# Decoder of two layers: the norms of the first cross attention moved to ScalarE, one turn later in the windowed attention, and the token shift of the last layer by transfers

## The chip, the cores and the metric

The kernel runs on one core of one Trainium2 chip. The metric is the device time of one execution in microseconds (us), the median of several runs. The engines of the core are TensorE (PE, with its weight loads PEld), VectorE (DVE), ScalarE (ACT), GpSimd (POOL) and SyncE (SP, which here only issues transfers).

## The reference

A post-norm decoder with two layers computes on `x` of 4 x 512 tokens of 128 features, with a context of 4 x 32 tokens. `_layernorm` subtracts the mean of the features and divides by the root of the variance plus 1e-5.

```
x = _layernorm(x + mamba(x))               # selective scan
x = _layernorm(x + cross_attention_0(x, ctx))
x = _layernorm(x + moe(x))                 # a shared expert and 2 of 8
x = _layernorm(x + windowed_attention(x))  # 16 heads, window 128
x = _layernorm(x + cross_attention_1(x, ctx))
x = _layernorm(x + local_layers(x))        # 2 layers, window 64
```

Three parts matter here. The first cross attention normalizes its input, attends with 16 heads to 32 context tokens, and adds a gated result:

```
xn = layernorm(x) * ln_gamma + ln_beta
out = softmax((xn @ w_q) . k * scale) . v @ w_out + b_out
x = _layernorm(x + out * tanh(gate))
```

The windowed attention gives for each tile of tokens an output by features, with the sum of the weights beside it, by which it is divided. Each of the two local layers has a feed-forward part that begins with a token shift and a norm:

```
def shift_token(t):
    t1, t2 = jnp.split(t, 2, axis=-1)
    t2 = jnp.pad(t2, ((0, 0), (1, 0), (0, 0)))[:, :-1]
    return jnp.concatenate([t1, t2], axis=-1)

h = shift_token(x); h = layernorm(h) * lg + lb
x = x + ffn(h)
```

So the second half of the features of a token comes from the token before it.

## The kernel before, in words

Tokens lie on the 128 partitions, 16 tiles of 128 tokens (`NT`), four tiles (`NJ`) to a batch; the features lie along the row. A matmul needs its contraction on the partitions, so tiles are turned by TensorE (`TE.transpose` with `ident`) into PSUM and copied from there by ScalarE or VectorE. All three parts are written in `tc.manual_schedule()`: each engine takes its instructions in about the order in which the code issues them, short ones slipped between long ones, and an engine that meets an instruction whose input is late stands still with all that is queued behind it.

*First cross attention* (`xa` pool, lines 971 to 1095). Each step `k` of 19 runs `tile_a(k)` and `tile_b(k)`: score of tile `k+1`, largest and exponentials of `k`, sums and products of `k-1`, turn and values of `k-2`, result of `k-3`. Beside these the next batch is prepared: `stats_x` (mean and variance of a tile on VectorE, `bn_stats`, `bn_aggr`, and `ve`, variance plus 1e-5; then the root `rs` on GpSimd by `rpow`, line 157, and `xr`, the residual plus bias, line 977), `norm_x` (line 985, VectorE: subtract the mean, multiply by the root; line 986: turn into `ptx`), and behind the fourth tile `xT` (ScalarE, line 989). Batch 0 is prepared in the stage before. `result` (line 1031) adds the residual and takes `stats` of the sum, `norm_r` (line 1036, VectorE) writes the normalized tile to `x2`. `exponentials` uses ScalarE (line 1004), `sums` multiplies by the inverse on GpSimd (`xpr`, line 1013), `turned_` turns that (`pt`, line 1019) and copies it on ScalarE (`xpT`, line 1021). A list `aside` adds the routing of the experts and the shared expert (`ph`, `w2s`) to the later steps; GpSimd then scatters the tokens of the first half to their experts (`xs`, line 818), and the first `fetch` of the experts (`xg`, turned in `ptg`, line 912) waits for all 16 scatters.

*Windowed attention* (lines 1157 to 1360). Step `s` takes four heads of tile `s // 4`. It issues `scores(s+1)` (`psc`, and VectorE's `nm`, line 1243), `tails(s, 0)`, `exponentials(s+1)` (`pe`, ScalarE, line 1250), `weights(s)` (turn `ptp`, line 1260, then `pT`, line 1262, one half on VectorE and one on ScalarE), `values(s-1)` (`pa`), `tails(s, 1)`, and the preparation `made` of the next batch, among it the rotary matmuls `pq` at s mod 16 of 5, 6, 7 and 9. `tails` finishes the tile before in four steps: `gathered` (ScalarE, `ao`, line 1280), `by_tokens` (turn `pn`, line 1288; inverse `rc`, line 1291; product `at`, line 1293), `by_features` with `output`, and `normed`. `pn`, `pto`, `po`, `pq` and `pv` share one PSUM buffer (tag `pm`).

*Last layer* (lines 1391 to 1792). Step `g` takes half the heads of tile `g // 2`; `around` and `feed` are lists of what else is issued at the three places of a step: the projections `pqk` and `pv` with the transfers `vh<-va` on SP (lines 1426 and 1428), the rotary parts on VectorE and GpSimd, the turns `ptk` (line 1485) and `ptq` (line 1476), the output `po` and its sum `xa` (VectorE, line 1561), and the feed-forward of the batch before. That begins with `ff_shift`: `shifted` turns the four tiles of `xa` to features (`pts`, line 1799); ScalarE copies the first 64 features (`hT`, line 1801) and VectorE the other 64, one token later (line 1802). One place later `ff_tokens` turns it back (`pth`, line 1578; copy to `hn`, line 1580). Then come `ff_stats` (with `rs` and two products `mr` on GpSimd, lines 157, 198, 199), `ff_norm` (ScalarE, line 209), `ff_features`, `ff_gates`, `ff_hidden` (`pff`, `ge`) and `ff_out` (`pof`). The last of the 8 turns of two layers and four batches runs alone behind the loop. The turns, `po`, `pv` and `pff` share three PSUM buffers (tag `pt`).

Helpers that the change uses: `shifts(mv, rs)` computes minus mean times root for four tiles on GpSimd, and `normal(x, mv, rs, of, mr)` normalizes four tiles by four ScalarE activations with that as bias and the root as scale.

Of the kernel before, what the change touches and what calls it, by code (L numbers as in the profile page):

```python
# [11 lines left out]
F32 = mybir.dt.float32  # L12
BF16 = mybir.dt.bfloat16
I32 = mybir.dt.int32
AF = mybir.ActivationFunctionType
ALU = mybir.AluOpType
# [3 lines left out]
P = 128  # L20
B, T, D = 4, 512, 128
NJ = T // P
# [35 lines left out]
def decoder_kernel(ctx: ExitStack, tc: tile.TileContext, a: dict):  # L58
    nc = tc.nc
    V, S, G, TE = nc.vector, nc.scalar, nc.gpsimd, nc.tensor  # L60
# [32 lines left out]
    def vcol(name, i=0):  # L93
        o = _VEC[name][0] + i
        return vec[:, o:o + 1]
# [59 lines left out]
    def rpow(out, in_, n):  # L155

        G.tensor_tensor(out, in_, cneg.to_broadcast([P, n]), ALU.pow)  # L157

    def stats(src):

        st = sm.tile([P, 6], F32, tag="st", name="st")
        V.bn_stats(st, src)
        mv = sm.tile([P, 2], F32, tag="mv", name="mv")
        V.bn_aggr(mv, st)
        ve = sm.tile([P, 1], F32, tag="ve", name="ve")
        V.tensor_scalar_add(ve, mv[:, 1:2], 1e-5)  # L166
        rs = sm.tile([P, 1], F32, tag="rs", name="rs")
        rpow(rs, ve, 1)
        return mv, rs
# [25 lines left out]
    def shifts(mv, rs):  # L195

        mr = sm.tile([P, NJ], F32, tag="mr", name="mr")
        G.tensor_tensor(mr, mv[:, :, 0], rs, ALU.mult)
        G.tensor_tensor(mr, mr, cminus.to_broadcast([P, NJ]), ALU.mult)
        return mr  # L200
# [715 lines left out]
    def weights(hf, t):  # L916

        ex = nc.values_load(which[hf][0:1, t:t + 1], engines=[mybir.EngineType.DVE], min_val=0, max_val=7,
                            skip_runtime_bounds_check_because="a minimum bounds the number by 7")
        wts[hf, t] = gp.tile([P, 2, 512], F32, tag="wt", name="wt", bufs=3)  # L920
        V.tensor_copy(wts[hf, t], w12[:, bass.ds(ex, 1)].rearrange("p o w h -> p (o w) h"))
# [47 lines left out]
            store(hf, g)  # L969

    with tc.tile_pool(name="xa", bufs=3) as t1:
        xrs, mvs, ptx, xTs, scs, mxs, xes, rcs, prs, xpTs, rs_ = ({} for _ in range(11))

        def stats_x(i):
            mvs[i] = stats(x1[:, i, :])
            xrs[i] = t1.tile([P, D], F32, tag="xr", name="xr", bufs=8)
            G.tensor_tensor(xrs[i], x1[:, i, :], gb, ALU.add)

        def norm_x(i):
            b, j = divmod(i, NJ)  # L980
            if j == 0:
                ptx[b] = ps.tile([P, NJ, P], F32, tag="ph", name="ptx")
            mv, rs = mvs.pop(i)
            xn = t1.tile([P, D], F32, tag="xn", name="xn")
            V.tensor_scalar(xn, x1[:, i, :], mv[:, 0:1], rs, ALU.subtract, ALU.mult)
            TE.transpose(ptx[b][:, j, :], xn, ident)
            if j == NJ - 1:
                xTs[b] = t1.tile([P, T], F32, tag="xT", name="xT", bufs=2)
                S.activation(xTs[b], ptx.pop(b).rearrange("p j t -> p (j t)"), AF.Identity,
                             bias=vcol("ln_b"), scale=vcol("ln_g"))  # L990

        def score(i):
            b, j = divmod(i, NJ)
# [35 lines left out]
        def result(i):  # L1029
            r = rs_[i] = t1.tile([P, D], F32, tag="r", name="r")  # L1030
            V.scalar_tensor_tensor(r, pos_.pop(i), gate, xrs.pop(i), ALU.mult, ALU.add)
            mvs["r", i] = stats(r)

        def norm_r(i):
            mv, rs = mvs.pop(("r", i))
            V.tensor_scalar(x2[:, i, :], rs_.pop(i), mv[:, 0:1], rs, ALU.subtract, ALU.mult)

        def tile_a(k):

            nxt = (k // NJ + 1) * NJ  # L1040
            if k + 1 < NT:
                score(k + 1)
            if 0 <= k - 2 < NT:
                turned_(k - 2)
            if k < NT:
                largest(k)
            if 0 <= k - 3 < NT:
                result(k - 3)
            if nxt < NT:
                for j in ((0, 1), (2, 3), (), ())[k % NJ]:  # L1050
                    stats_x(nxt + j)

        def tile_b(k):
            nxt = (k // NJ + 1) * NJ
            if k < NT:
                exponentials(k)
            if 0 <= k - 1 < NT:
                sums(k - 1)
            if 0 <= k - 3 < NT:
                norm_r(k - 3)  # L1060
            if 0 <= k - 2 < NT:
                values(k - 2)
            if nxt < NT:
                for j in ((), (0, 1), (2, 3), ())[k % NJ]:
                    norm_x(nxt + j)


        aside = {(7, 1): [(turn, 0)], (8, 1): [(shared_first, 0)], (9, 1): [(shared_second, 0), (shared_add, 0)],
# [88 lines left out]
    with tc.tile_pool(name="wa", bufs=2) as bp, tc.tile_pool(name="wa_p", bufs=2) as t1, \  # L1157
# [150 lines left out]
        def normed(i):  # L1308
# [4 lines left out]
        made = {3: [(turn_x,)], 5: [(rotary, 0, 0)], 6: [(rotary, 0, 1)], 7: [(rotary, 1, 0)], 9: [(rotary, 1, 1)],  # L1313
                10: [(head_values,)], 11: [(head_keys, 0), (head_keys, 1)], 12: [(head_keys, 2), (head_keys, 3)],
                13: [(head_keys, 4), (head_keys, 5)], 14: [(head_keys, 6), (head_keys, 7)]}
        tail = [[None, gathered], [by_tokens, None], [by_features, output], [normed, None]]

        def tails(s, k):
            i = s // 4 - 1
            f = tail[s % 4][k]  # L1320
            if f and i >= 0:
                f(i)

        with tc.manual_schedule():
            beside = {3: [(blocks_x, 1)], 5: [(g_x, 0)], 6: [(g_x, 1)], 7: [(g_x, 2)], 9: [(g_x, 3)], 10: [(v_x, 0), (v_x, 1)],
                      11: [(v_x, 2)], 12: [(v_x, 3)]}
            blocks_x(0)
            for t in sorted(made):
                for f, *c in made[t]:
                    f(0, *c)  # L1330
                for f, *c in beside.get(t, []):
                    f(*c)
            scores(0)
            exponentials(0)
            last = 4 * NT
            for s in range(last):
                if s + 1 < last:
                    scores(s + 1)
                tails(s, 0)
                if s + 1 < last:  # L1340
                    exponentials(s + 1)
                weights(s)

                if s < HT_:
                    for q in range(2):
                        gather(1, 2 * s + q)
                if s % 2 == 0 and 4 <= s < 4 + 2 * HT_:
                    combined(1, s // 2 - 2)
                if s % 2 and 4 <= s < 4 + 2 * HT_:
                    norm_3(1, s // 2 - 2)  # L1350
                if s:
                    values(s - 1)
                tails(s, 1)
                if s // 16 + 1 < B:
                    for f, *c in made.get(s % 16, []):
                        f(s // 16 + 1, *c)
            values(last - 1)
            for s in range(last, last + 4):
                tails(s, 0)
                tails(s, 1)  # L1360

    kept.close()

# [27 lines left out]
    with tc.tile_pool(name="la_b", bufs=2) as bp, tc.tile_pool(name="la_t", bufs=2) as t1, \  # L1391
# [1 line left out]
            tc.tile_pool(name="la_ps", bufs=2, space=PSUM) as ps:  # L1393


        hTz = [bp.tile([P, T], F32, tag=f"hT{k}", name=f"hT{k}", bufs=1) for k in range(3)]
        for k in hTz:
            V.memset(k[64:128, 0:1], 0.0)
        va = bp.tile([P, NJ, 8, 65], F32, tag="va", name="va", bufs=1)
# [5 lines left out]
        ins = [x5]  # L1405
        hTs, pqks, tas, tbs, rns, sss, qTs, pes, pTs, ats, aTs = ({} for _ in range(11))
        xTs, xes, xps, xpTs = ({} for _ in range(4))
        xas, h2s, hns, hnTs, xabs, ges, mvs, fins = ({} for _ in range(8))


        def shift(b):
# [149 lines left out]
            V.tensor_tensor(xas[i // NJ][:, i % NJ, :], po, ins[i // NT][:, i % NT, :], ALU.add)  # L1561

        def ff_shift(q):
            l, b = divmod(q, B)
            xa = xas.pop(q)
            h2s[q] = hTz[2]
            shifted(nc, ps, xa, 0, h2s[q], ident, 3)
            xabs[q] = bp.tile([P, NJ, D], F32, tag="xab", name="xab", bufs=2)
            G.tensor_tensor(xabs[q], xa,
                            rcol("f_b2", 128 * l, 128).unsqueeze(1).to_broadcast([P, NJ, D]), ALU.add)  # L1570
            if l == 1:
                G.tensor_tensor(xabs[q], xabs[q], x5[:, b * NJ:(b + 1) * NJ, :], ALU.add)

        def ff_tokens(q):
            pt = ps.tile([P, NJ, P], F32, tag="pt", name="pth", bufs=3)
            hT = h2s.pop(q)
            for j in range(NJ):
                TE.transpose(pt[:, j, :], hT[:, j * P:(j + 1) * P], ident)
            hns[q] = bp.tile([P, NJ, D], F32, tag="hn", name="hn", bufs=1)
            S.copy(hns[q], pt)  # L1580

        def ff_stats(q):
            mv, rs = stats4(hns[q])
# [114 lines left out]
        def x_norm(b):  # L1698
# [14 lines left out]

        feed = {(0, 0): [[], [], [(ff_hidden, 2, 0)]], (0, 1): [[], [(ff_hidden, 2, 1)], []],
                (1, 0): [[(ff_shift, 1)], [(ff_hidden, 2, 2)], []],
                (1, 1): [[(ff_tokens, 1)], [], []],
                (2, 0): [[(ff_stats, 1)], [(ff_out, 2)], []],
                (2, 1): [[], [], [(ff_norm, 1)]],
                (3, 0): [[(last_stats, 2)], [], []],
# [11 lines left out]
        with tc.manual_schedule():  # L1731
# [46 lines left out]
            ff_shift(e)  # L1778
            for c in range(3):
                ff_hidden(e - 1, c)  # L1780
            ff_tokens(e)
            ff_stats(e)
            ff_out(e - 1)
            ff_norm(e)
# [10 lines left out]
def shifted(nc, ps, x, b, hT, ident, bufs):  # L1795

    pt = ps.tile([P, NJ, P], F32, tag="pt", name="pts", bufs=bufs)
    for j in range(NJ):
        nc.tensor.transpose(pt[:, j, :], x[:, b * NJ + j, :], ident)
    pf = pt.rearrange("p j t -> p (j t)")  # L1800
    nc.scalar.copy(hT[0:64, :], pf[0:64, :])
    nc.vector.tensor_copy(hT[64:128, 1:T], pf[64:128, 0:T - 1])
# [131 lines left out]
```

## Time and profile before

| | |
|---|---|
| three runs | 1275.3, 1281.07 and 1281.63 us, median 1281.07 |
| the profiled execution | 1280.2 us, span from the first to the last instruction 1278.5 us |
| mean granted clock of TensorE | 0.943 |
| busy in the span | PE 1100.2 us (86%), PEld 712.8 (56%), DVE 910.4 (71%), ACT 729.9 (57%), POOL 638.2 (50%) |
| chain that ended last, by engine | PE 49%, DVE 16%, ACT 6%, POOL 2%, issue 2% |

The stages that the change touches lie at about 315 to 425 us (first cross attention), 556 to 800 (windowed attention) and 870 to 1278 (last layer). A busy time counts what an engine does, not what bounds the stage: that is read from the waits (engine, line, what released it) and from the chain, which is followed back from the last instruction to what released each. A duration in a view by lines is a mean over all of that line's shapes.

### The profile page before, as it was taken

How to read it: one execution, taken by the hardware profiler on the slowest of the kernel's cores; microseconds unless marked ns; L12 is line 12 of the kernel's file. 1: busy time of each engine (PE TensorE's matmuls, PEld its weight loads, DVE VectorE, ACT ScalarE, POOL GpSimd, SP SyncE). 2: the span in 40 equal slices, each digit the busy share in tenths (PEclk: the TensorE clock that was granted, in tenths of full speed). 3: DMA queues.
4: the chain of work that ended last, by engine and by line, in shares of the span. 5: the costliest groups of instructions: out<-in, count | busy, mean ns of one | idle time of the engine just before them, and what ended most of it. 6: DMA issues, size and time to landing. Idle time of an engine off the chain costs nothing.

```text
span 1278.5 us, 22122 instructions
## 1 busy us (share of the span) xinstructions
PE 1100.2 (86%) x8429; PEld 712.8 (56%) x8429; DVE 910.4 (71%) x1722; ACT 729.9 (57%) x1612; POOL 638.2 (50%) x509
## 2 busy tenths in 40 slices
PE   4879888787698789988898998778999999999985
PEld 1334433343366779855555565446666566666563
DVE  3889898897876556847866666687777667766743
ACT  5696958662353445544656565346676665665752
POOL 3568675864546143433110100467785666676621
PEclk9799989897798899989999999899999999999997
DMA  9000000001200612200000000000110100110100
GB/s 270 1 0 1 1 0 1 1 0 65 84 1 30 228 63 80 63 22 14 2 1 2 2 2 2 0 9 21 28 23 14 27 22 15 26 23 14 35 14 17
DMA packets 34573, 38.92 MB, mean 30 GB/s; under 512 B 3378, under 2 KB 25667, under 8 KB 33987
## 3 DMA queue, kind: packets, MB, share of 16 engines
q1 hardware_dynamic: 31874, 31.69, 8.6%
q0 software_dynamic: 2048, 4.20, 1.1%
q10 hardware_dynamic: 544, 1.62, 0.5%
q8 instruction: 66, 1.08, 0.4%
q14 instruction: 41, 0.33, 0.1%
HBM read 20.80 MB, written 9.18 MB: 23 GB/s over the span
## 4 chain that ended last, share of the span: by engine, by line
PE 49%; DVE 16%; ACT 6%; issue 2%; POOL 2%; DMA 0%; DVEq 0%; ACTq 0%; POOLq 0%; SPq 0%
PE psc L189 9%; PE pa L189 4%; PE pqk L189 4%; PE pff L189 3%; PE po L189 3%; PE ptp L1260 3%; PE phg L189 3%; PE pog L189 2%; PE pv L189 2%; PE pof L189 2%; PE ptp L1527 1%; ACT pe L1250 1%; PE ptq L1476 1%; PE pq L189 1%; DVE nm L1243 1%
## 5 line engine op out<-in xcount | busy, mean ns | idle before, releaser
L440 POOL TENSOR_TENSOR h<-h,cb 128x1024 f32<-128x1024 f32 (+1 forms) x65 | 151.8, 2338 | 66.3 <-DVE h L435 49.8
L157 POOL TENSOR_TENSOR rs<-ve,cneg 128x1 f32<-128x1 f32 (+1 forms) x81 | 59.0, 728 | 232.5 <-DVE ve L166 193.8
L435 DVE TENSOR_TENSOR_SCAN h<-dA,pb 128x1024 f32<-128x1024 f32 x64 | 146.4, 2287 | 18.5 <-ACT dA L427 4.9
L1250 ACT ACTIVATE pe<-psc,nm 128x256 f32<-128x256 f32 (+1 forms) x256 | 93.6, 449 | 73.1 <-DVE nm L1243 72.8
L189 PE MATMUL y<-h,ident 128*128 128x512 f32 x256 | 127.2, 620 | 5.4 <-POOL h L440 4.7
L1458 POOL TENSOR_TENSOR ta<-ta,tb 128x1024 f32<-128x1024 f32 x32 | 75.4, 2357 | 111.6 <-DVE rc L1542 65.1
L1243 DVE TENSOR_REDUCE nm<-psc 128x4 f32<-128x1024 f32 (+1 forms) x64 | 69.8, 1091 | 56.7 <-PE psc L189 49.8
L157 POOL TENSOR_TENSOR rn<-ss,cneg 128x16 f32<-128x16 f32 x32 | 93.0, 2906 | 0.0
L1512 DVE TENSOR_REDUCE nm<-psc 128x4 f32<-128x512 f32 x64 | 44.0, 687 | 64.4 <-PE psc L189 62.7
L427 ACT ACTIVATE dA<-delta,negA 128x512 f32<-128x512 f32 (+1 forms) x128 | 85.3, 715 | 4.7 <-POOL delta L346 4.4
L189 PEld LDWEIGHTS y<-h,ident 128*128 128x128 f32 x256 | 49.6, 198 | 65.1 <-issue 46.5
L929 ACT ACTIVATE hTg<-phg,bias 128x128 f32<-128x128 f32 x184 | 52.7, 368 | 57.9 <-PE phg L189 57.2
L432 DVE TENSOR_TENSOR pb<-du,pb 128x1024 f32<-128x1024 f32 x64 | 77.5, 1211 | 2.7 <-PE pb L189 2.2
L1521 ACT ACTIVATE pe<-psc,nm 128x128 f32<-128x128 f32 x256 | 73.8, 381 | 5.4 <-DVE nm L1512 5.3
L189 PE MATMUL pb<-stk,sel 96*128 96x512 bf16 x128 | 41.5, 408 | 32.7 <-DVE h L435 15.5
L1260 PE MATMUL ptp<-ident,pe 128*128 128x128 f32 x448 | 64.5, 281 | 4.8 <-ACT pT L1262 2.0
L189 PE MATMUL pqk<-f_qkv,hT 128*128 128x512 f32 x128 | 64.9, 631 | 4.1 <-DVE tb L1452 4.0
L189 PE MATMUL psc<-kb,qk 64*128 64x256 f32 (+1 forms) x512 | 67.1, 381 | 0.0
L1466 POOL TENSOR_TENSOR ta<-ta,rn 128x1024 f32<-128x1024 f32 x32 | 60.9, 1903 | 2.4
L1260 PEld LDWEIGHTS ptp<-ident,pe 128*128 128x128 f32 x448 | 49.8, 142 | 16.9 <-issue 6.7
L189 PEld LDWEIGHTS <-sel 96*128 96x128 bf16 x192 | 18.9, 103 | 69.3 <-issue 42.3
L1432 ACT ACTIVATE sq<-pqk 128x1024 f32<-128x1024 f32 x32 | 32.9, 1029 | 42.8 <-PE pqk L189 35.3
(375 smaller groups left out, 2879.6 us busy)
## 6 DMA issues: line engine op xcount, KB each, us to landing
vh<-va SPq DMA_DIRECT2D x56, 130.0 KB, 2.3
w<-in_e_w_dram SPq DMA_DIRECT2D x16, 256.0 KB, 5.2
xs<-zero SPq DMA_DIRECT2D x2, 1472.0 KB, 12.7
xg<-xs SPq DMA_DIRECT2D x10, 256.0 KB, 3.1
ys<-yg SPq DMA_DIRECT2D x10, 256.0 KB, 2.4
f_qkv<-in_f_qkv_dram SPq DMA_DIRECT2D x1, 1536.0 KB, 6.6
x<-in_x_dram SPq DMA_DIRECT2D x4, 256.0 KB, 10.8
w_kv<-in_w_kv_dram SPq DMA_DIRECT2D x1, 1024.0 KB, 8.1
```

The source lines that it names most:

```text
L157: G.tensor_tensor(out, in_, cneg.to_broadcast([P, n]), ALU.pow)
L189: TE.matmul(out, lhsT=lhsT, rhs=rhs, start=start, stop=stop)
L427: S.activation(dAs[k % 4][:, c, c:T], delta[b % 2][:, c, c:T], AF.Exp, scale=negA[:, c * NST + n:c * NST + n + 1])
L432: V.tensor_tensor(pb, du[steps[k][0] % 2], pb, ALU.mult)
L435: V.tensor_tensor_scan(h.rearrange("p c t -> p (c t)"), dAs[k % 4].rearrange("p c t -> p (c t)"), pb.rearrange("p c t -> p (c t)"), 0.0, A ...
L440: G.tensor_tensor(h[:, c], h[:, c], cb.unsqueeze(1).to_broadcast([P, n, T]), ALU.mult)
L1243: V.tensor_reduce(nm, psc[:, :, 0:nk], AX.X, ALU.max, negate=True)
L1250: S.activation(pe[:, h, 0:nk], psc[:, h, 0:nk], AF.Exp, bias=nm[:, h:h + 1])
L1260: TE.transpose(ptp[:, h * nb + kk, :], pe[:, 2 * pr + h, kk * P:(kk + 1) * P], ident)
L1458: G.tensor_tensor(ta, ta, tbs.pop(i).rearrange("p w h d -> p (w h) d"), ALU.add)
L1466: G.tensor_tensor(ta, ta, rns.pop(i).unsqueeze(2).to_broadcast([P, 16, 64]), ALU.mult)
L1521: S.activation(pes[g][:, h, :], o[:, par, q, :], AF.Exp, bias=nm[:, k:k + 1])
```

## The change

Three edits in one. First cross attention: `stats_x` keeps mean and variance of the four tiles of a batch in one tile and takes one root and one `shifts` for all four behind the last; `norm_x` does a whole batch by `normal` on ScalarE at `tile_b` of the batch's second step, and the turn becomes `turn_x`, issued at `tile_a` of the third. The result's norm goes to ScalarE, with minus mean times root from two one-column products on GpSimd.

```
 def stats_x(i):
-    mvs[i] = stats(x1[:, i, :])
+    b, j = divmod(i, NJ)
+    if j == 0:
+        mvs[b] = sm.tile([P, NJ, 2], F32, tag="mv4", name="mv4")
+    st = sm.tile([P, 6], F32, tag="st", name="st")
+    V.bn_stats(st, x1[:, i, :])
+    V.bn_aggr(mvs[b][:, j, :], st)
     xrs[i] = t1.tile([P, D], F32, tag="xr", name="xr", bufs=8)
     G.tensor_tensor(xrs[i], x1[:, i, :], gb, ALU.add)
+    if j == NJ - 1:
+        ve = sm.tile([P, NJ], F32, tag="ve4", name="ve4")
+        V.tensor_tensor(ve, mvs[b][:, :, 1], eps.to_broadcast([P, NJ]), ALU.add)
+        rs = sm.tile([P, NJ], F32, tag="rs4", name="rs4")
+        rpow(rs, ve, NJ)
+        mvs[b] = mvs[b], rs, x1[:, b * NJ:(b + 1) * NJ, :], shifts(mvs[b], rs)

-def norm_x(i):
...
-    V.tensor_scalar(xn, x1[:, i, :], mv[:, 0:1], rs, ALU.subtract, ALU.mult)
-    TE.transpose(ptx[b][:, j, :], xn, ident)
...
+def norm_x(b):
+    xns_[b] = t1.tile([P, NJ, D], F32, tag="xn", name="xn", bufs=1)
+    normal(xns_[b], *mvs.pop(b))
+
+def turn_x(b):
+    pt = ps.tile([P, NJ, P], F32, tag="ph", name="ptx")
+    xn = xns_.pop(b)
+    for j in range(NJ):
+        TE.transpose(pt[:, j, :], xn[:, j, :], ident)
+    xTs[b] = t1.tile([P, T], F32, tag="xT", name="xT", bufs=2)
+    S.activation(xTs[b], pt.rearrange("p j t -> p (j t)"), AF.Identity, bias=vcol("ln_b"), scale=vcol("ln_g"))

 def result(i):
...
-    mvs["r", i] = stats(r)
+    mv, rs = stats(r)
+    mr = sm.tile([P, 1], F32, tag="mr1", name="mr1")
+    G.tensor_tensor(mr, mv[:, 0:1], rs, ALU.mult)
+    G.tensor_tensor(mr, mr, cminus, ALU.mult)
+    mvs["r", i] = mr, rs

 def norm_r(i):
-    V.tensor_scalar(x2[:, i, :], rs_.pop(i), mv[:, 0:1], rs, ALU.subtract, ALU.mult)
+    S.activation(x2[:, i, :], rs_.pop(i), AF.Identity, bias=mr, scale=rs)

 # tile_a
+        if k % NJ == 2:
+            turn_x(nxt // NJ)
 # tile_b
-        for j in ((), (0, 1), (2, 3), ())[k % NJ]:
-            norm_x(nxt + j)
+        if k % NJ == 1:
+            norm_x(nxt // NJ)
```

Windowed attention: `tails` has three places in a step, and `by_tokens` moves to the new one, behind `weights(s)` and ahead of `values(s-1)`.

```
-tail = [[None, gathered], [by_tokens, None], [by_features, output], [normed, None]]
+tail = [[None, None, gathered], [None, by_tokens, None], [by_features, None, output], [normed, None, None]]

 weights(s)
+tails(s, 1)
...
 values(s - 1)
-tails(s, 1)
+tails(s, 2)
```

Last layer: `ff_shift` writes the shifted tokens straight to `hn`, the second half of the features by two transfers on SP from partition to partition, the first half by a ScalarE copy; `ff_tokens` is gone, and `hn` has two buffers. The third `hT` buffer is gone. (The turns for the attention's own shift, `shift`, stay.)

```
 def ff_shift(q):
     l, b = divmod(q, B)
     xa = xas.pop(q)
-    h2s[q] = hTz[2]
-    shifted(nc, ps, xa, 0, h2s[q], ident, 3)
+    hn = hns[q] = bp.tile([P, NJ, D], F32, tag="hn", name="hn", bufs=2)
+    nc.sync.dma_start(hn[1:P, :, 64:D], xa[0:P - 1, :, 64:D])
+    nc.sync.dma_start(hn[0:1, 1:NJ, 64:D], xa[P - 1:P, 0:NJ - 1, 64:D])
+    G.memset(hn[0:1, 0, 64:D], 0.0)
+    S.copy(hn[:, :, 0:64], xa[:, :, 0:64])
...
-def ff_tokens(q):
-    pt = ps.tile([P, NJ, P], F32, tag="pt", name="pth", bufs=3)
-    hT = h2s.pop(q)
-    for j in range(NJ):
-        TE.transpose(pt[:, j, :], hT[:, j * P:(j + 1) * P], ident)
-    hns[q] = bp.tile([P, NJ, D], F32, tag="hn", name="hn", bufs=1)
-    S.copy(hns[q], pt)
...
-        (1, 1): [[(ff_tokens, 1)], [], []],
```

## The prediction, made before the change was run

> **What bounds the kernel now.** The changed code runs in three stages, so the first view is the busy time by stage (columns: stretch, its length, busy us of PE, its weight loads, VectorE, ScalarE and GpSimd, granted clock, DMA share):
>
> ```profile
> 300.00:430.00 130.00, 103.09 (x488) 70.24 (x487) 90.18 (x283) 45.44 (x78) 61.97 (x88) 0.82 0.19 62
> ...
> 650.00:700.00 50.00, 45.03 (x497) 29.81 (x496) 33.07 (x62) 30.76 (x84) 4.82 (x9) 1.00 0.01 1
> ...
> 940.00:1010.00 70.00, 66.17 (x659) 43.89 (x658) 47.54 (x95) 46.82 (x102) 47.33 (x26) 1.00 0.10 22
> ```
>
> In the first cross attention (300 to 430) no engine is full: PE 79%, VectorE 69%. It is a relay of short waits. In the windowed attention (556 to 800) PE is busy 90% with gaps, and in the last layer (870 to 1245) 95%: there every matmul taken away counts almost in full. Next the waits of the first two stages (engine, line, released by: us, times, longest):
>
> ```profile
> DVE x L1036 <- POOL rs L157: 13.1, 9, 6.1
> ```
>
> ```profile
> PE ptx L986 <- DVE xn L985: 3.7, 3, 2.3
> ```
>
> ```profile
> PE pn L1288 <- ACT ao L1280: 11.3, 12, 1.2
> ```
>
> The first two are of 305 to 430, the third of 556 to 790. VectorE stands for GpSimd's root before the result's norm; PE stands for ScalarE's copy of the attention output before turning it to tokens. Last the chain that ends latest, one place of each of the two later stages (start, us, what):
>
> ```profile
> 574.23 1.20 ACT pe L1250 x3
> 575.43 0.48 ACT pT L1262
> 575.91 0.50 ACT ao L1280
> 576.45 0.66 PE pn L1288 x4
> 577.10 0.87 PE ptp L1260 x8
> ```
>
> ```profile
> 1016.57 0.49 PE pts L1799 x3
> ...
> 1017.40 0.34 PE pts L1799
> ...
> 1017.77 0.45 ACT hT L1801
> 1018.22 0.04 issue
> 1018.26 0.59 ACT pT L1529
> ...
> 1018.90 0.66 PE ptq L1476 x4
> ```
>
> In the first, `ptp` needs only `pe`, done at 575.43, but stands in PE's order behind `pn`, which needs `ao`. In the second the turn of `xa` for the token shift holds PE, then ScalarE, and through `pT` also `ptq`.
>
> **Part 1, norms of the first cross attention (300 to 430).** Removed from VectorE: 12 `xn` (4.5 us), 16 `x` L1036 (9.1 us, mean 570 ns), 9 of 12 `ve` of the tokens (0.15 each, 1.3 us), and the standing for `rs` (13.1). On the chain these rows are: `xn`, its turn and `xT` at the two batch boundaries, 328.72 to 331.39 and 349.09 to 351.00 (2.7 and 1.9 us); `rs` ahead of a result four times (0.52, 0.56, 0.52, 0.57: 2.2 us); L1036 eight times (0.35, 1.06, 1.06, 0.23, 0.35, 0.29, 1.06, 0.26: 4.7 us). That is 11.4 us, the end of the gain. The other end is a loss, for what is added: 28 ScalarE activations at 0.48 (the L209 rows; 13.4 us, in a stage with 85 us of ScalarE idle), and on GpSimd three four-wide roots (1.03 at 319.14) for twelve of 0.55, three pairs at 0.2 (L198 and L199 at 1253.62) and 16 pairs of one column, not in this trace; I take 0.2 each from those four-column rows, between 0.07 (the smallest row here, a memset on VectorE) and 0.55 (the one-column root): 6.4 us. Two of these pairs stand between the 16 scatters at 394 to 418, where GpSimd issues without pause and the expert fetch waits for the last one: 0.8 us of loss in plain sight. The new wait is ScalarE's for `rs` and `mr`: the four `xn` of a batch stand ahead of `xpT` and `xT`, so the first `xpT`, now at 325.46, comes about when GpSimd has done four `xr`, root and pair (some 325.1) plus four activations (1.65): 326.8, 1.3 us late, and the first boundary gains some 1.8 us, not 2.7. And between 358 and 378 PE has hardly a gap (`ph` 3.60, `w2s` 3.74), so what VectorE saves there is hidden. In the tail two turns of `xpr` now stand ahead of `w2s` on PE instead of one behind it; that shift fits into the 3.9 us for which PE stands at `ptg` for the fetch. I take half of 11.4 less 0.8: **5 us**, between a gain of 11 and a loss of 3 (two boundaries at 1.3, no gain).
>
> **Part 2, `by_tokens` behind `weights` (556 to 800).** No instruction more or less; `pn` and its two VectorE rows (`rc` 0.26, `at` 0.29) move behind `ptp` and the `pT` copies. At the place shown `ptp` would run 575.5 to 576.4, `pn` right behind it when `ao` is there, `pa` at 577.1 instead of 577.98: 0.9 us, near the mean wait, 11.3 / 12. But `pn` shares its one PSUM buffer with the next batch's rotary matmul `pq`, which in 6 of 16 tiles comes directly behind `pa`; it then waits for `at`, now queued behind `nm` and `pT` on VectorE: about 578.25 against 578.48 before, 0.2 us gained. So 12 x 10/16 x 0.9 + 12 x 6/16 x 0.2 = 7.7; **7.5 us**, between 1.5 (the copy stays late) and 11.3.
>
> **Part 3, the shift by transfers (870 to 1260).** Per batch and layer go: four `pts` (0.44 to 0.6 as a group), `hT` on ScalarE (0.58) and VectorE (0.69), four `pth` (0.44), the `hn` copy (0.59). Come: two transfers on SP, a memset of one row on GpSimd (nobody needs it before `st`), one ScalarE copy of 128x256, 0.39 by the 128x256 `pT` row. Seven of eight are in the loop. At 1016.57 PE would go on with `ptp` (0.60), `ptk` (0.44), `ptq` (0.66) and end at 1018.27, not 1019.56: 1.29 gained; the next `pff` may wait 0.2 for `pT`, behind the copy that itself waits for `xa` (1017.36). With `pth` 0.44, whose place is pure PE work, 1.55 x 7 = 10.9. If `ptq` still waits for `pT` (some 1018.4) it is 0.94 x 7 = 6.6; the upper end is 1.73 x 7 = 12.1. The nearer row is a step without a shift: `ptk` 894.80, `ptq` 895.25, no wait. So 11.
> What hides the transfers: `ff_stats` reads `hn` a whole tile later (934.5, against `xa` at 923.4). The nearest row is `vh<-va`, SBUF to SBUF, 130 KB in 64 long rows, 2.3 us; this one has the same bytes in 508 rows of 256 B. By the page, queue 1 spent 8.6% of 16 x 1278.5 us on 31874 packets, 55 ns each; 508 / 16 of them are 1.8 us, so I estimate 3.5 to 4.1 us to landing. On SP the `vh` transfers are queued behind it; the next is issued at 932.5, nine us later.
> The last batch has no such cover: `xa` at 1245.3, landing about 1249.2. VectorE, with `pff` started 0.9 us earlier, finishes `ge` near 1249.3 where `st` began at 1250.56 before: 1.1 us, nothing if the landing is a microsecond later. Part 3: **12 us**, between 6 and 14.
> The Trainium skill ("DMA: Bandwidth & Descriptors", Specifications) says that transfers need at least 512 B for line rate, and below it the engine reads, modifies and writes; these rows have 256 B. If that doubled the 2.3 us and more, the loop's eleven us of cover would still hide it, and only the 1.1 us at the end would go: 1257 for 1256. Its section on small descriptors confines the penalty to HBM; no row here shows 256 B rows between SBUF tiles.
>
> **Sum.** 5 + 7.5 + 12 = 24.5. The profiled execution took 1280.2 us (span 1278.5), 0.9 under the median of the three runs, 1281.07. 1280.2 - 24.5 = **1256 us**.
>
> **Rivals.**
> *ScalarE becomes the queue (slower).* In stage 1 each norm on ScalarE stands until GpSimd delivers, and `xpT` and `exp` stand behind it, which PE needs next. For: VectorE stood up to 6.1 us for one such root, between scatters. Against: most of those waits were 0.4 to 0.5 us, and the instruction ahead is usually an `exp` of 0.63 that covers them. It decides from about 1.6 us per result, seen by PE's `po` each time: 16 x 1.6 = 26 lost instead of 5 gained, and with the other parts' 19.5 the time is 1287.
> *PE is not the bound where it is freed.* VectorE's run `nm`, `ta`, `ss`, `tb` (907 to 913) or the late `pT` sets the pace; parts 2 and 3 give 1.5 and 6.6: 1267. For: `pff` waits 7.3 us for `tb`. Against: 95% PE in that stage.
> *The relay of stage 1 gives nothing* (bound by PE and the scatters): 1261.
> *More of the chain goes:* 8 in stage 1, 11.3 and 14 behind it, 33.3 in all: 1247.
>
> **Chances.** Forecast (1251 to 1260) 0.50; stage 1 nothing 0.15; PE not the bound 0.14; more 0.07; the two middle rivals at once, 1272 and up to 1284 when stage 1 loses its 3 and the rest is nearly nothing, 0.09; ScalarE's queue 0.05. The range is 1246 to 1272, leaving out the last two and half of "more". A measurement of this kernel can tell about 0.5%, 6.4 us, from no change. Faster by more (under 1274.7): the first four and some of the fifth, 0.88; within: 0.07; slower: 0.05.
>
> **What would show it.** Stage 1 by its waits: no VectorE row standing for `rs`, PE not standing for `xn`, the first scatter some 6 us earlier; wrong if ScalarE's norms show standing and `po <- xpT` (5.4 us now) has grown. Stage 2: `pn <- ao` under 3 us in all, and `pq` waiting for `at` in six tiles. Stage 3: no `pts` of `xa`, `ptq` straight behind `ptk`, `st` never waiting for a transfer in the loop, the period of 48.7 us per batch down to 47.1. Wrong altogether if PE's busy time falls by these 7 us and the stage keeps its length.

## The result, and the profile after

The changed kernel takes 1259.62 us (median of 6 runs, 1257.41 to 1262.20) against 1278.92 for the kernel before beside it (6 runs): ratio 0.985, 95% interval 0.983 to 0.987. The forecast was 1256 with a range of 1246 to 1272, so sign and size were right. The sum of 24.5 us came out as 19.3, or 21.5 between the spans of the two profiled executions (1278.5 and 1257.0), and one term had the wrong sign.

The busy view by stages, cut at the same instructions in both traces (length in us, and the granted clock beside it):

| stretch | before | after |
|---|---|---|
| start to the first score `sc` (not edited) | 315.0 at 0.93 | 316.8 at 0.92 |
| first score `sc` to first scatter `xs` (part 1) | 79.5 at 0.84 | 75.5 at 0.90 |
| to the first turned fetch `ptg` | 28.1 at 0.80 | 28.5 at 0.82 |
| to the windowed attention's first `psc` (not edited) | 133.7 at 0.94 | 130.0 at 0.99 |
| to the next attention's first `psc` (part 2) | 243.5 at 0.98 | 231.9 at 0.99 |
| to the last layer's first `psc` (not edited) | 72.3 at 0.88 | 74.4 at 0.82 |
| to the last `xa` (part 3, seven of eight batches) | 372.9 at 0.99 | 362.1 at 1.00 |
| to the end (part 3, the last batch) | 33.5 at 0.75 | 37.8 at 0.73 |

The three stretches that nobody edited moved by 1.8 up, 3.7 down and 2.1 up, each with its granted clock. So a difference between two traces is an edit's only at the same clock.

Part 1. The waits of the changed kernel between 305 and 421 us (engine, line, released by: us, times, longest):

```profile
ACT x L1050 <- POOL mr L1045: 19.2, 9, 5.5
...
PE pt L1029 <- POOL xpr L1023: 8.2, 4, 2.9
...
ACT xn L209 <- POOL mr L199: 6.4, 3, 3.4
...
PE po L189 <- ACT xpT L1031: 5.4, 7, 1.0
```

VectorE no longer stands for the root; ScalarE stands in its place, for GpSimd's products. PE's wait for `xpT` has not grown, so that standing is cheap. What has grown is PE's wait for GpSimd's `xpr`; in the kernel before (305 to 430 us) it was

```profile
PE pt L1019 <- POOL xpr L1013: 2.7, 2, 1.4
```

Run e7 asks whether the new products are the reason.

Part 2. The waits of the changed kernel between 553 and 800 us:

```profile
PE pq L189 <- DVE at L1309: 2.2, 6, 0.5
...
PE pn L1304 <- ACT ao L1296: 0.7, 1, 0.7
```

`pn` stood 11.3 us for `ao` and stands 0.7; six times `pq` waits for `at`, which shares its buffer. In the chain of the changed kernel one such place reads (start, us, what):

```profile
568.32 0.17 DVE rc L1307
568.49 0.02 issue
568.51 0.30 DVE at L1309
568.82 0.14 issue
568.95 1.10 PE pq L189 x2
```

`ao` is gone from the chain; the new queue behind VectorE's inverse and product is the one foreseen.

Part 3. The chain of the changed kernel at one of the batches in the loop, and at the last one:

```profile
999.49 0.29 DVE xa L1578
999.78 0.02 issue
999.80 0.02 ACT hn L1588
999.83 0.29 issue
1000.11 0.59 ACT pT L1546
1000.70 0.04 issue
1000.75 1.09 PE pff L189 x2
```

```profile
1219.16 0.30 DVE xa L1578
1219.52 9.11 DMA hn<-xa
...
1228.75 0.31 DVE st L176
```

In the loop no turn of `xa` is left, and `pff` goes behind `pT`, which goes behind the copy to `hn`. At the end the chain stands 9.11 us on the transfer. The instructions on `hn` of the changed kernel (duration in ns: least, median, most) and its DMA view between 1222 and 1226 us say why:

```profile
L1585 SPq DMA_DIRECT2D hn<-xa x8: 732/755/806, 908.4 to 1219.5; - x8
...
L1586 SPq DMA_DIRECT2D hn<-xa x8: 6420/6463/6524, 909.2 to 1220.3; - x8
```

```profile
DMA packets 278, 0.07 MB, mean 18 GB/s; under 512 B 278, under 2 KB 278, under 8 KB 278
...
q1 hardware_dynamic: 278, 0.07, 7.8%
```

The second transfer has three rows, yet holds SP for 6.4 us: it stands behind the first. In 4 us 278 packets pass, one every 14.4 ns, and the 16 DMA engines are busy 7.8%, little over one engine's share of 6.25%. By the packet records of the trace each takes 18 ns and at most 3 are under way at once; of the rows of `vh<-va` 17 are. So the rows are not slow. They go nearly one after another.

### The profile page after: what moved, and what is told of

It reads as the page before. It is cut to its first block, busy times and chain, and to the rows that moved or that the text cites. A ratio compares the mean times of both kernels' runs of the same rounds, so it can differ in the third digit from the quotient of the medians.

```text
span 1257.0 us, 22080 instructions
## 1 busy us (share of the span) xinstructions
PE 1085.9 (86%) x8365; PEld 698.0 (56%) x8365; DVE 890.8 (71%) x1676; ACT 735.1 (58%) x1632; POOL 643.3 (51%) x546
## 4 chain that ended last, share of the span: by engine, by line
PE 44%; DVE 20%; ACT 4%; issue 3%; POOL 2%; DMA 1%; DVEq 0%; ACTq 0%; POOLq 0%; SPq 0%
PE psc L189 9%; PE pqk L189 4%; PE pa L189 4%; PE po L189 3%; PE ptp L1276 3%; PE pff L189 3%; PE phg L189 3%; PE pog L189 2%; DVE tb L1469 2%; PE pv L189 2%; DVE ss L1455 2%; DVE ta L1462 2%; PE pof L189 1%; DMA hn<-xa 1%; PE pq L189 1%
## 5 line engine op out<-in xcount | busy, mean ns | idle before, releaser
L157 POOL TENSOR_TENSOR rs<-ve,cneg 128x1 f32<-128x1 f32 (+1 forms) x72 | 55.0, 764 | 217.7 <-DVE ve L166 175.9
L1475 POOL TENSOR_TENSOR ta<-ta,tb 128x1024 f32<-128x1024 f32 x32 | 75.5, 2358 | 103.7 <-DVE rc L1559 51.0
L432 DVE TENSOR_TENSOR pb<-du,pb 128x1024 f32<-128x1024 f32 x64 | 77.5, 1211 | 2.9 <-PE pb L189 2.2
L189 PE MATMUL pb<-stk,sel 96*128 96x512 bf16 x128 | 41.6, 408 | 32.7 <-DVE h L435 15.5
L189 PE MATMUL pff<-hnT,f_w 128*128 128x512 f32 (+1 forms) x96 | 50.4, 645 | 9.8 <-DVE tb L1469 7.3
```

The lines of the kernel that those rows point to most:

```text
L189: TE.matmul(out, lhsT=lhsT, rhs=rhs, start=start, stop=stop)
L432: V.tensor_tensor(pb, du[steps[k][0] % 2], pb, ALU.mult)
L1475: G.tensor_tensor(ta, ta, tbs.pop(i).rearrange("p w h d -> p (w h) d"), ALU.add)
```

## The experiments

Every kernel of this section ran beside runs of the kernel before on its chip. Those 47 runs spread from 1267.9 to 1284.1 us while their mean granted clock went from 0.957 to 0.941, some 0.9 us for each 0.001. A difference called "at equal clock" is from one fit over the runs of all kernels but e6, with a constant for each kernel and one slope (0.84 us for each 0.001); the ± is 95%. The fit has a weakness: an edit can move the mean clock itself. The end of the changed kernel is 37.8 us at 0.73, that of e5 31.8 at 0.79; over a whole run this is some 0.003 of the mean clock, and at 0.84 us for each 0.001 the fit books some 2 us of e5's gain as clock (an estimate from these four numbers). Where an edit touches the end, the stretches of the traces tell more.

**Each edit alone.** e1, e2 and e3 are the kernel before with one of the three hunks of the diff shown above.

> The kernel before with the first edit alone: both norms of the first cross attention. Theory: each edit is worth what its own stage lost between the two traces, and the differences in stages that were not edited (+1.8, -3.7 and +2.0 us) go with the granted clock and not with an edit. From the first score to the first fetched turn that is 3.6 us less, so about 1275.3 against 1278.9, ratio 0.997. Rival A, my forecast of 5: 1273.9. Rival B, the norms brought nothing and the 3.6 are the clock too (0.92 to 0.97 in the next stretch): 1278.9, and the stretch from the first score to the first scatter stays at 79.5 us instead of 75.6.

Measured: 1270.41 us, ratio 0.993 (0.991 to 0.995); at equal clock 2.8 ± 1.2 less. From the first score to the first scatter it is 78.2 us at a clock of 0.82. The old code needs 79.5 at 0.84 and, in e3, 78.0 at 0.88; the new one 78.2 at 0.82 and 75.5 at 0.90, by a straight line 77.5 at 0.84 and 76.2 at 0.88. Later traces with the same code there have 74.7 at 0.88 (e9) and 74.5 at 0.90 (e10). So the edit is worth 2 to 3.4 us there, and up to half of the 3.6 between the first two traces is clock. Rival B falls, and so does my forecast of 5.

> The kernel before with the second edit alone: the turn of the attention output to tokens issued behind the turn of the weights. Theory: the whole 11.6 us that the windowed attention lost (243.3 to 231.7 from its first to the other stage's first score) come from this edit, since PE no longer stands for the copy (11.3 us before, 0.7 after): about 1267.3, ratio 0.991. Rival, my forecast: 7.5 us, 1271.4, with the other 4 from a better clock in that stretch; then this run's stretch is about 235.8 at the clock of before.

Measured: 1268.88 us, ratio 0.994 (0.992 to 0.997); at equal clock 7.3 ± 1.0 less. Its windowed attention takes 237.9 us at 0.97, too low a clock for a comparison. At 0.98 the old order takes 243.5 (kernel before) and 242.7 (e3), the new one 235.0 (e8) and 235.5 (e11), 7 to 8.5 less. The forecast of 7.5 stands, and the theory of 11.6 falls: those two traces had clock in them.

> The kernel before with the third edit alone: the shift of the last layer by transfers. Theory: the loop gives 10.7 us (372.7 to 362.0) and the last batch gives 4.3 back (33.5 to 37.8), since its transfer lands 9 us after xa and nothing covers that: 1272.5, ratio 0.995. Rival A, my forecast, landing in 4 us: 12 less, 1266.9. Rival B, the 4.3 at the end are clock or chance and not the transfer: the end is 33.5 again and the time 1268.

Measured: 1270.78 us, ratio 0.996 (0.993 to 0.999); by the fit 7.3 ± 1.0 less. The loop is 362.0 us at 1.00, against 371.4 at 1.00 in e1: 9.4 gained. The end is 37.5, against 32.5 to 33.5 in the three kernels with the old shift: 4 to 5 lost, so some 5 are left by the stretches. The theory holds, and both rivals fall. By the fit the three edits add up to 17.4, the whole change to 16.7 ± 1.0: that they disturb each other does not show within the error.

**The last batch.** In e4 the last of the eight batches turns as before:

```
+if q == 2 * B - 1:
+    shifted(nc, ps, xa, 0, hTz[0], ident, 3)    # and ff_tokens(q) behind the loop
+else:
     (the two transfers, the memset and the copy)
```

> The changed kernel, except that the last of the eight batches is shifted by the two turns through features as before; the seven in the loop keep their transfers. Theory: the end goes back to 33.5 us or a little under, the loop stays at 362: 4.3 to 5.4 less than the changed kernel's 1259.6, that is 1254.2 to 1255.3. Rival, the longer end is not the transfer's: 1259.6. Second rival, the transfer's queue in the loop is what feeds the gain at the end, so that the loop changes as well: its stretch moves by over 1 us.

Measured: 1254.20 us, ratio 0.981 (0.978 to 0.984); by the fit 4.1 ± 1.6 under the changed kernel. The end is 31.8 us, the loop 361.9. The longer end is the transfer's, and the loop does not depend on what is done at the end.

**Why the transfer takes 9 us.** Three kernels change its form. e5:

```
-nc.sync.dma_start(hn[1:P, :, 64:D], xa[0:P - 1, :, 64:D])
+nc.sync.dma_start(hn[1:113, :, 64:D], xa[0:112, :, 64:D])
+nc.sync.dma_start(hn[113:P, :, 64:D], xa[112:P - 1, :, 64:D])
```

> The changed kernel, with the shift's first transfer cut in two: 112 partitions and 15 partitions instead of 127; rows, bytes and tiles are the same, only one more issue. In the changed kernel's trace the 508 rows of 256 B go one after another: one starts every 14.6 ns, at most 3 are under way at once, and they need 7.4 us, while each takes only 18 ns; of the two-part vh transfers (64 rows of 2080 B each) 17 are under way at once. Theory A: a transfer over 127 partitions is served by one DMA engine, because 127 has no divisor up to 16 but one; 112 has 16, and 15 has 15. Then the rows land in some 3 to 4 us, the last batch's statistics begin when VectorE is free, 4.4 us earlier, and the time is about 1255.2 against the changed kernel's 1259.6. The Trainium skill (DMA: Bandwidth & Descriptors, Why a DMA increments its semaphore by 16 and not by 1) states such a rule: as many of 16 engines as divide the slowest dimension of both sides. Theory B: rows of 256 B are slow whoever serves them: landing stays at 9.1 us, 1259.6. Theory C: SP's queue feeds the rows one by one at 14.6 ns: landing 9.1 plus one issue of 0.75, 1260.3.

Measured: 1253.72 us, ratio 0.984 (0.981 to 0.987); by the fit 3.6 ± 1.5 under the changed kernel, the end 31.8 us and so 6.0 shorter. The issues of e5 (KB each, median us to landing), the instructions on `hn`, and its chain at the last batch:

```profile
vh<-va SPq DMA_DIRECT2D x56, 130.0 KB, 2.3
hn<-xa SPq DMA_DIRECT2D x8, 112.0 KB, 2.4
hn<-xa SPq DMA_DIRECT2D x8, 15.0 KB, 2.2
```

```profile
L1586 SPq DMA_DIRECT2D hn<-xa x8: 938/942/1474, 909.9 to 1220.9; - x8
```

```profile
1219.80 2.59 PE pff L189 x6
...
1222.49 0.64 DVE ge L1631
...
1223.27 0.31 DVE st L176
```

Line 1586 is the transfer of 15 partitions here. The same rows of 256 B land like the long ones of `vh`, up to 22 packets are under way at once, and the transfer has left the chain: `st` now follows VectorE's `ge`, as the forecast had it for the changed kernel. Theories B and C are out.

e6 goes the other way, fewer and longer rows on 127 partitions. It also puts ScalarE's copy behind the transfer:

```
-nc.sync.dma_start(hn[1:P, :, 64:D], xa[0:P - 1, :, 64:D])
+nc.sync.dma_start(hn[1:P], xa[0:P - 1])      # and the copy of [0:64] ahead of the statistics
```

> The changed kernel, with whole rows sent: 127 partitions with one contiguous row of 2 KB each instead of 508 rows of 256 B, four times fewer rows and twice the bytes; ScalarE's copy of the first halves then goes ahead of the statistics. Theory A (one engine serves 127 partitions): a packet of 2080 B takes 0.145 us in this kernel's trace, so 127 of 2048 B one after another are up to 18 us, longer than the eleven us of cover in the loop; landing 18 to 20 us after xa, the end 9 us longer than the changed kernel's, and the loop loses as well: 1268 or more. If packets follow each other faster on one engine, landing is between 9 and 18. Theory B (short rows): no row is under 512 B, landing about 3 us, 1255. Theory C (14.6 ns a row from SP): 127 rows are 1.9 us, landing 3.7 us, 1255.

Measured: 1305.65 us, ratio 1.024 (1.020 to 1.027), slower than the kernel before. Its chain at the last batch, and a wait of its last layer:

```profile
1258.89 0.66 SPq L1585
1259.55 0.05 issue
1259.60 12.81 DMA hn<-xa
```

```profile
ACT hn L1598 <- DMA hn<-xa: 57.4, 8, 15.2
```

127 packets of 2 KB go at most 2 at once, one every 91 ns, 11.6 us in all. That is more than the loop's eleven us of cover once the fixed part is added, so now all eight batches wait for it (57.4 us), where the changed kernel waited twice. The wait is ScalarE's, which holds all that is queued behind the copy, so the loop's loss is not the transfer's length alone. Theory A had both signs; its 18 us were too many, because a packet of 2 KB took 84 ns here (median) and not the 145 of the rows of `vh`.

e10 asks whether the divisor matters, or any cut in two:

```
-hn[1:113] <- xa[0:112], hn[113:P] <- xa[112:P - 1]
+hn[1:123] <- xa[0:122], hn[123:P] <- xa[122:P - 1]
```

> The changed kernel, with the shift's first transfer cut into 122 and 5 partitions instead of 112 and 15. Theory A (a transfer is served by as many DMA engines, up to 16, as divide its partitions): 122 has only the divisor 2, so 488 rows go by two engines, 3.6 us at 14.6 ns a row and engine instead of 7.4 by one and about 1.1 to 1.8 by sixteen; the statistics of the last batch begin some 5.2 to 6 us after xa (3.5 with 112 and 15, 9.2 with 127 in one), and the last stretch is 33.5 to 34.5 us (31.8 and 37.8). Rival A: any cut into two transfers brings it, since two issues are served side by side, or the cure is that no transfer is longer than some number of partitions: then 112 and 122 behave alike or 122 like 127: statistics at 3.5 or 9.2. The Trainium skill (DMA: Bandwidth & Descriptors, Why a DMA increments its semaphore by 16 and not by 1) has the rule of the divisors.

Measured: 1256.36 us, ratio 0.986 (0.981 to 0.992), too wide to place the kernel by its time; the trace does. The instructions on `hn` of e10, and its chain at the last batch:

```profile
L1586 SPq DMA_DIRECT2D hn<-xa x8: 2767/2842/2857, 909.4 to 1220.5; - x8
```

```profile
1219.39 0.30 DVE xa L1578
...
1220.55 4.87 DMA hn<-xa
1225.61 0.30 DVE st L176
```

Line 1586 is the transfer of 5 partitions here. One row every 7.5 ns, 3.9 us in all: half of what 127 partitions need, twice what 112 and 15 need (1.8). SP stands 2.8 us where it stood 6.4 and 0.9. The statistics begin 6.2 us after `xa`, the end is 33.9 us. Rival A is out. The pace goes with the largest divisor up to 16: 1 for 127, 2 for 122, 16 for 112. So rows seem to go by as many lanes. Sixteen lanes are not sixteen times as fast, though: the 448 rows of the 112 partitions start within 0.8 us, one every 1.8 ns, an eighth of 14.5, and what sets the pace there is not shown. The traces count the lanes as well. When the rows have landed, the transfer's semaphore is raised once in the changed kernel (at 1228.63 us) and in e6 (1272.24), twice in e10 (1225.23 and 1225.24) and sixteen times in e5 (1222.33 to 1222.70, for the 112 partitions). That these lanes are DMA engines is the Trainium skill's account (DMA: Bandwidth & Descriptors, Why a DMA increments its semaphore by 16 and not by 1): of 16 engines as many serve a transfer as divide the slowest dimension of both sides. The counts of 1, 2 and 16 agree with it; no row here names an engine.

**Why part 1 brought 2 to 3 and not 5.** e7 takes `mr` to VectorE, e8 the whole norm of the result:

```
 e7, in result:
-G.tensor_tensor(mr, mv[:, 0:1], rs, ALU.mult)
-G.tensor_tensor(mr, mr, cminus, ALU.mult)
+V.scalar_tensor_tensor(mr, mv[:, 0:1], -1.0, rs, ALU.mult, ALU.mult)
 e8, no mr, and in norm_r:
-S.activation(x2[:, i, :], rs_.pop(i), AF.Identity, bias=mr, scale=rs)
+V.tensor_scalar(x2[:, i, :], rs_.pop(i), mv[:, 0:1], rs, ALU.subtract, ALU.mult)
```

> The changed kernel, with minus mean times root of the first cross attention's result by one VectorE operation instead of two GpSimd products (16 pairs of 0.19 + 0.19 us, 6.1 us of GpSimd). Theory: the relay there is now paced by GpSimd, whose xpr has 8.2 us of the chain (5.2 before) and for which PE stands 8.2 us; without the pairs each xpr comes 0.4 us earlier where a pair lies ahead of it, two scatters follow sooner (0.8), and the stretch from the first score to the first scatter falls from 78.2 (at a granted clock of 0.82) or 75.5 (at 0.90) by 1.5 to 3; the time falls to about 1257.5. Rival: PE and the chain through largest, difference and exponentials set that stretch; nothing changes there, 1259.6. Second rival: the operation on VectorE waits for the root and holds VectorE as the normalization did in the kernel before (13 us in all): the stretch grows by up to 2, 1261.5.

Measured: 1258.00 us, ratio 0.986 (0.983 to 0.989); at equal clock 0.9 ± 1.5 under the changed kernel. Its stretch to the first scatter is 77.1 us at 0.84, where the line above gives 77.5, and between 314 and 394 us PE stands 4.8 us for `xpr`, 4.9 in the changed kernel. Taking 16 pairs of products off GpSimd changes nothing that can be measured: the theory that they pace the stage falls, and the 1.5 to 3 with it.

> The changed kernel, with the result's norm of the first cross attention back on VectorE (subtract, multiply) as before the change; the tokens' norm stays on ScalarE by four tiles. Theory: the first edit is worth some 2 us, and they are those of the two batch boundaries, where the new statistics, root and four ScalarE activations replace four VectorE normalizations; the result's norm on ScalarE brings what it costs, since ScalarE stands 19 us for the products mr of GpSimd and the products delay xpr: time equal to the changed kernel within 1 us, 1259.6. Rival A: the result's norm is where the 2 us come from, 1261.6 here, and VectorE stands again for the root. Rival B: it is a loss hidden in the sum, 1258 here.

Measured: 1256.90 us, ratio 0.986 (0.983 to 0.989); at equal clock 1.0 ± 1.5 under the changed kernel; 75.2 us at 0.88. At that clock e11, with the same norm on VectorE, takes 74.7, and so does e9, with the norm on ScalarE. So the result's norm may sit on either engine, and what part 1 brings is left for the tokens' norm at the two batch boundaries; no run moves that norm alone. Rival A falls; of rival B (a small hidden loss) the stretches show nothing, but it is within the error of the times.

**Control and combination.** e9 is the changed kernel again; e11 has the cut of e5 and the norm of e8.

> The changed kernel itself once more, on the same chip and beside the same runs of the kernel before as the next two, so that their differences to it are had without the clock of another session. Runs of the kernel before spread from 1268 to 1284 us with the granted clock (0.957 to 0.941), some 0.9 us for each 0.001. Expected: 17 us less than before at equal clock, the last stretch from xa to the end at 37.5 to 38 us. Rival: the 19.3 us measured first were all the edits', and the difference is 19 to 20 at equal clock too.

Measured: 1258.45 us, ratio 0.986 (0.982 to 0.990); with the first six runs 16.7 ± 1.0 less than before at equal clock, the end 37.8 us. The rest of the first 19.3 goes with the clock, as far as the fit can tell.

> The version that the runs point to: the changed kernel with the transfer cut into 112 and 15 partitions and the result's norm of the first cross attention back on VectorE. Theory: the last stretch 31.8 us as with the cut alone, the first cross attention as in the changed kernel: 4 to 6 us under the changed kernel of this call at equal clock, about 1253 to 1255. Rival: the cut gains at the end but the transfers in the loop, now on all engines, collide with vh, so that the loop loses 1 to 2 us: 1256.

Measured: 1251.08 us, ratio 0.980 (0.976 to 0.984); by the fit 4.9 ± 1.6 under the changed kernel. Loop 361.6 us, end 31.6: no collision with `vh`. It has the shortest time here; e4 and e5 lie within the error of it.

## Why the prediction was right, and where it was wrong

*Part 1, 5 us forecast, 2.8 ± 1.2 measured.* Mis-sized was the term "half of 11.4". Its rows of the chain were read rightly, but those of the result (4.7 for L1036 and 2.2 for the root) were not earned: with that norm on VectorE again (e8) or on ScalarE the stage is as long, and VectorE's standing of 4.9 us for the root in e8 costs nothing. What is left is the boundaries' part (1.8 for the first). The sign that I named, the first scatter six us earlier, was 4 counted from the first score, of which up to 2 were clock. The other signs held: no VectorE row for the root, PE 0.6 us for `xn` (3.7 before), `po` no worse. Rival "ScalarE becomes the queue" was right in its mechanism, 19.2 us of standing, and wrong in its price, since PE's `po` never saw it.

*Part 2, 7.5 forecast, 7.3 ± 1.0 measured.* The place-by-place reading held: PE no longer stands for `ao`, and six tiles are caught by `pq` behind `at`. The 0.9 for each of the other ten was not measured tile by tile.

*Part 3, loop, 10.9 forecast, 9.4 measured.* The freed turns count nearly in full. The period of a batch is 47.4 us (`hn` copies at 999.8 and 1047.2), 47.1 forecast. `ptq` is no longer released by `pT` but for 1.8 us; the new link is `pff` behind `pT` behind the copy, which I had at 0.2.

*Part 3, last batch, 1.1 gained forecast, 4 to 5 lost measured: this is the step that failed.* "508 / 16 of them are 1.8 us, so I estimate 3.5 to 4.1 us to landing" spread the rows over 16 engines, as the share of queue 1 is counted over 16. The landing took 9.1. With rows that are served side by side (e5) it takes 2.4, the statistics follow `ge`, and the end is 31.8 at 0.79, where the old shift takes 32.7 at 0.79 (e1), 0.9 better: the rest of the step was right. In the loop the cover of eleven us hid 9.1 as it was meant to hide 4, except for one wait of 1.0 where I had written "never".

The rule that I weighed from the Trainium skill (DMA: Bandwidth & Descriptors, Specifications), read-modify-write below 512 B, was not the cause: a row of 256 B takes 18 ns in the changed kernel and in e5, and 2.4 us for 112 KB is what the long rows need. The doubling that I weighed with it, at a price of the 1.1 us alone, was too small as well: the landing took four times the 2.3 us of the nearest row.

*The sum.* The 24.5 of the three parts became 17.4 by the fit of the edits alone, and 14 to 17 by the stretches (2 to 3.4, 7 to 8.5, some 5). That the medians show 19.3 goes with the clock of those runs, as far as the fit can tell: part of the nearness to 1256 is luck. With 16.7 off the profiled 1280.2 the time would be 1263.5, still within the range.

## What to carry to other kernels

Count the partitions of a transfer before you price it: 127 of them went one row at a time, and a cut into 112 and 15 turned 9.1 us to landing into 2.4 with one more issue (2.9 until the second piece had landed too). Price a moved transfer where it has no cover, the last turn of a loop, not where it has. And compare two traces stage by stage with the granted clock beside each: what moves in a stage that nobody edited shows how far a difference can be something other than the edit. The mean clock of a whole run does not replace this, since an edit that lets PE wait can lower it.

## What the runs showed of the hardware that was not expected

- A transfer between tiles on chip ran at a pace set by its number of partitions: a row of 256 B every 14.5 ns with 127, every 7.5 with 122, every 3.6 with 112 and 15, the pause between the two included; a row of 2 KB every 91 ns with 127. At the end its semaphore was raised 1, 2 or 16 times (127, 122, 112).
- A slow transfer holds its queue, but not until it has landed: the one issued next kept SP 6.4 us (three rows, behind 127 partitions), 2.8 (5 partitions, behind 122) or 0.9 (15 partitions, behind 112), and 4.0 us behind the 2 KB rows of e6, whose landing took 13.0. In the changed kernel SP came free at 1226.7 us, when some 110 rows had still to start.
- One and the same kernel took 1267.9 to 1284.1 us, in step with a mean granted clock of 0.957 to 0.941, so that differences of 5 us need the clock beside them.
